# Graph-network stack on one core: the second hop's weights folded into the first's, its node features made by VectorE transposes

## The chip, the cores and the metric

One NeuronCore of one Trainium2 chip runs the kernel. The metric is device microseconds from start to end of an execution. The kernel before took 709.7 us, the median of three runs from 709.64 to 709.86.

## The reference

The input is 3327 nodes with 64 features and a sparse weighted matrix adj of 3327 x 3327 in float32. Four residual layers follow each other; each takes a layer norm and a relu of x, runs its own graph network on it, and adds the result to x. Together they multiply by a matrix made from adj eight times. These eight sweeps are numbered k = 0 to 7 in the kernel. The change concerns the third layer, sweeps k = 3, 4 and 5:

```python
w = left_weights * A                      # both are adj: the squares of adj
for W, b in ((W0, b0), (W1, b1), (W2, b2)):
    x = w @ x
    x = x @ W.T + b
```

The other sweeps are two gated graph units (k = 0, 1, on adj itself), a ranked-neighbour layer (k = 2, on weights made from a mask of adj) and two dense hops with tanh (k = 6, 7, on adj itself).

## The kernel before

**Tiling.** The nodes are padded to 26 blocks of 128 and split in two halves of 13 blocks, s = 0 and 1, which lie side by side on the partition axis: features of half 0 on partitions 0 to 63, of half 1 on 64 to 127. The 13 block positions are cut into four chunks c = 0 to 3 of 3, 3, 3 and 4 blocks, so 384, 384, 384 and 512 columns. Chunks 0 and 1 are group 0, chunks 2 and 3 are group 1. [...]One tile holds one block of 128 source nodes against one group of target nodes: 768 KB for group 0, 896 KB for group 1. Twenty slots hold such tiles, and SyncE's DMA queue fills them (L369).

**Sweeps.** For one source tile and one target chunk, a "unit", TensorE runs in L571 two products, one for each half. Each is shown by the profile as two matmul instructions, since the data are float32. A unit accumulates into a "sum" bank of PSUM, transposed: features on partitions, target nodes on columns. When the last source has been added, the chunk's task after_k starts. Two sweeps share one reading of a tile (`joint`): the order is k = 3 for group 1 beside k = 2, then k = 3 and 4 for group 0, k = 4 and 5 for group 1, k = 5 and 6 for group 0, k = 6 and 7 for group 1, and k = 7 for group 0.

**Order of the work.** The program is a fixed order for each engine, written by a planner. `run` goes through the units, issues loads ahead, prepares the squares six units ahead, and expands the ranked weights three units ahead. After each unit `spend` hands its estimated duration (0.86 us for 512 columns) to the open tasks; a task is a generator whose `yield` says how long to let pass before its next instructions are put into the queues. Nothing is timed on the chip itself: an instruction runs when those before it on its engine are done and its semaphores are there.

**Squares.** For k = 3 to 5, `square` (L402 to L406) squares a tile in place or into a spare half slot. Two of three go to ScalarE (L404). The third goes to VectorE (L406) only if no chunk has an open task; otherwise ScalarE does it too.

**The ranked sweep.** For k = 2 each unit needs a product of a mask with a triangular matrix (L271, `tri`) into a PSUM bank, which ScalarE (L487) or VectorE (L485) turns into weights `e`, before the three bfloat16 terms of the unit run on TensorE. These products, all tasks' products and the sums share the eight PSUM banks: `take` hands out the bank that was given back longest ago, and `give` returns it.

**After a hop.** In `after_hop(k)`, for k = 3 and 4, the sum is copied from PSUM to SBUF in `evacuate` (VectorE, L719, for chunks 0 and 2; ScalarE, L717, for 1 and 3). `dense_to_nodes` multiplies it by the hop's weights: two products for each block (helper `mm`, L271), with nodes on partitions as a result. VectorE adds the bias on its way back to SBUF (L929) and writes y of sweep k + 1, the operand of the next sweep. `bd` holds the weights of the ranked layer and of the three hops as block-diagonal 128 x 128 matrices, places 0 to 3; `brow` holds the three hops' biases as rows (0 to 2).

**Constants.** The task `more_constants` (L204 to L257) loads and builds weights during the first sweeps. Its last steps are the DMAs of bd (L250), w3 (L252) and brow (L254). `transpose_on_vector` (L760 to L769), which sweeps 6 and 7 use, transposes in 32 by 32 squares on VectorE: sixteen instructions of 32 partitions for a chunk.

Of the kernel before, what the change touches and what calls it, by code (L numbers as in the profile page):

```python
# [9 lines left out]
F32 = mybir.dt.float32  # L10
BF16 = mybir.dt.bfloat16
I16 = mybir.dt.int16
AF = mybir.ActivationFunctionType
ALU = mybir.AluOpType
# [30 lines left out]
N, D = 3327, 64  # L45
P = 128
# [8 lines left out]
CWM = 512  # L55
# [10 lines left out]
WL1, WL2, WL3 = 14, 15, 18  # L66
# [25 lines left out]
def upper(n):  # L92
    return slice(n * D, (n + 1) * D)
# [3 lines left out]
def kernel(  # L97
# [9 lines left out]
    nc = tc.nc  # L107

    const = ctx.enter_context(tc.tile_pool(name="const", bufs=1))
    feat = ctx.enter_context(tc.tile_pool(name="feat", bufs=2))  # L110
    work = ctx.enter_context(tc.tile_pool(name="work", bufs=4))
# [11 lines left out]
    bd = const.tile([P, 4, P], F32, name="bd")  # L123
# [5 lines left out]
    both += [both[1][:, :, (CH[c][0] - CH[1][0]) * P:(CH[c][1] - CH[1][0]) * P] for c in PARTS]  # L129
    bcol = const.tile([P, NBIAS], F32, name="bcol")  # L130
    brow = const.tile([P, 4, D], F32, name="brow")
    ident = const.tile([P, P], F32, name="ident")
    make_identity(nc, ident)
    tri = const.tile([P, P], BF16, name="tri")
# [15 lines left out]
    def load_cell(cell):  # L150
        nc.sync.dma_start(out=stage[upper(0), :7 * D].rearrange("p (w f) -> p w f", f=D),
                          in_=weights[:, (W1, W2)[cell]:(W1, W2)[cell] + 7])
        if cell == 0:
            nc.sync.dma_start(out=stage[upper(0), 7 * D:], in_=bias_cols)

    def unfold_cell(cell):

        n = 3 * D + (NBIAS if cell == 0 else 0)
        i, ps = take()
        for h in range(2):  # L160
            nc.tensor.matmul(ps[upper(h), :n], ident[:, :D], stage[:, 4 * D:4 * D + n], start=True, stop=True)
        v = ps[:, :3 * D].rearrange("p (g f) -> p g f", f=D)
        for h in range(2):
            nc.vector.tensor_copy(cells[upper(1 - h), cell, h, 0:3], v[upper(1 - h)])
        if cell == 0:
            nc.vector.tensor_copy(bcol, ps[:, 3 * D:n])
        give(i)

    def fold_cell(cell):

        i, ps = take()
        for n in range(2):
            for h in range(2):
                nc.tensor.matmul(ps[upper(h), upper(n)], stage[:, :D], ident[:, :D], start=True, stop=True)
        tr = work.tile([P, P], F32, name="t2")
        nc.scalar.copy(tr, ps[:, :P])
        give(i)
        yield 1.0
        i, ps = take()
        mm(ps[:, :3 * D], tr, stage[:, D:4 * D])  # L180
        v = ps[:, :3 * D].rearrange("p (g f) -> p g f", f=D)
        for h in range(2):
            nc.vector.tensor_copy(cells[upper(h), cell, h, 0:2], v[upper(h), 0:2])
            nc.vector.tensor_copy(cells[upper(h), cell, h, 3], v[upper(h), 2])
        give(i)
# [4 lines left out]
    def ahead_of_cell(c):  # L190
# [10 lines left out]
        nc.scalar.copy(ahead[c], ps[:, :width(c)])  # L201
        give(i)

    def more_constants():  # L204
        nc.gpsimd.memset(stage, 0.0)
        nc.gpsimd.memset(cells, 0.0)
        for c in range(NC):
            for h in range(2):
                nc.gpsimd.memset(both[c][upper(h), h], 0.0)
        nc.gpsimd.memset(bd, 0.0)  # L210
        yield 5.0
        load_cell(0)
        yield 20.0
        unfold_cell(0)
        yield 1.0

        full = work.tile([P, P], BF16, name="t2")
        nc.gpsimd.memset(full, -TWO7)
        nc.gpsimd.affine_select(out=tri, in_=full, pattern=[[-1, P]], compare_op=ALU.is_gt, fill=0.0,
                                base=0, channel_multiplier=1)  # L220
        nc.gpsimd.affine_select(out=tri, in_=tri, pattern=[[-1, P]], compare_op=ALU.not_equal, fill=TWO7 * TWO7,
                                base=0, channel_multiplier=1)
        nc.gpsimd.memset(tri[:, P - 1:P], 0.0)
        nc.gpsimd.memset(bitsb, BITS)
        nc.gpsimd.memset(lasty, 0.0)
        wide = work.tile([P, P], F32, name="t2")
        nc.gpsimd.memset(wide, 0.0)

        for i, (bi, bh) in enumerate(((BI1, BH1), (BI2, BH2))):
            nc.vector.tensor_add(bsum[:, i], bcol[:, bi:bi + 2], bcol[:, bh:bh + 2])  # L230

        nc.vector.tensor_scalar(wide[0:D], wide[0:D], bcol[0:D, BL1:BL1 + 1], None, op0=ALU.add)
        yield 3.0
        i, ps = take()
        mm(ps[:, :D], wide, ident[:, :D])
        nc.vector.tensor_copy(brow[:, 3], ps[:, :D])
        give(i)
        yield 1.0
        yield from fold_cell(0)
        for c in range(NC):  # L240
            yield 1.0
            ahead_of_cell(c)
        yield 50.0
        load_cell(1)
        yield 20.0
        unfold_cell(1)
        yield from fold_cell(1)
        yield 30.0
        for h in range(2):
            nc.sync.dma_start(out=bd[upper(h), :, upper(h)], in_=weights[:, WL1:WL3])  # L250
            for i in range(2):
                nc.sync.dma_start(out=w3[upper(h), :, i], in_=weights[:, WL3 + (h + i) % 2:NW:2])  # L252
        yield 5.0
        nc.sync.dma_start(  # L254
            out=brow[:, 0:3],
            in_=bass.AP(tensor=bias_rows.tensor, offset=bias_rows.offset, ap=[[0, P], [D, 3], [1, D]]),
        )  # L257


    def blocks(c):  # L260
        return CH[c][1] - CH[c][0]

    def width(c):
        return blocks(c) * P

    def mm(out, lhsT, rhs, start=True, stop=True):


        for h in range(2):
            hs = slice(h * D, (h + 1) * D)  # L270
            nc.tensor.matmul(out[hs], lhsT[:, hs], rhs, start=start, stop=stop)  # L271
# [8 lines left out]
    def take(sums=False, either=True):  # L280


        either = either and not sums
        pool = idle_sums if sums else idle_temps
        if either and idle_sums and (not pool or released[idle_sums[0]] < released[pool[0]]):
            pool = idle_sums
        for c in list(tasks):
            if not pool and c not in running:
                advance(c)
        i = pool.popleft()  # L290
        return i, banks[i]

    def give(i):
        released[i] = max(released) + 1
        (idle_sums if i < 4 else idle_temps).append(i)

    def nodes(c):

        return feat.tile([P, blocks(c), 2, D], F32, name=f"y{c}")
# [4 lines left out]
    def groups(t):  # L304
        return t.rearrange("p b s d -> p (b s) d")
# [4 lines left out]
    def view(ps, c):  # L310
        return ps[:, :width(c)].rearrange("p (b f) -> p b f", f=P)
# [5 lines left out]
    def advance(c):  # L317
        running.add(c)
        try:
            tasks[c][1] = next(tasks[c][0])  # L320
        except StopIteration:
            del tasks[c]
        running.discard(c)
# [23 lines left out]
    y = [[None] * NC for _ in range(8)]  # L347
    after = [None] * 8
# [365 lines left out]
    def evacuate(acc, c, busy=False):  # L714
        m = work.tile([P, CWM], F32, name="t2")[:, :width(c)]
        if c % 2 or busy:
            nc.scalar.copy(m, acc[0][1][:, :width(c)])  # L717
        else:
            nc.vector.tensor_copy(m, acc[0][1][:, :width(c)])  # L719
        give(acc[0][0])  # L720
        return m

    def dense_to_nodes(ft, w, c):

        i, ps = take()
        v = view(ps, c)
        for b in range(blocks(c)):
            mm(v[:, b, :], ft[:, b * P:(b + 1) * P], bd[:, w - WL1, :])
        return i, v
# [30 lines left out]
    def transpose_on_vector(h, c):  # L760

        for s in range(2):
            to = both[c][:, s].rearrange("p (b q n) -> p b q n", q=4, n=32)
            for q in range(4):
# [3 lines left out]
                if q % 2:  # L768
                    yield 1.5  # L769

    def evacuate_stacked(acc, c):
        nc.scalar.copy(both[c][upper(0), 0], acc[0][1][upper(0), :width(c)])  # L772
        nc.vector.tensor_copy(both[c][upper(1), 1], acc[1][1][upper(1), :width(c)])  # L773
        for i in {acc[0][0], acc[1][0]}:
            give(i)
# [142 lines left out]
        yield 15.0  # L918
        add_row(c, 2)

    def after_hop(k):
        def done(c, acc):
            m = evacuate(acc, c)
            yield 0.8
            v = dense_to_nodes(m, WL2 + k - 3, c)
            yield 0.8
            yk = nodes(c)
            n = 2 * blocks(c)
            nc.vector.tensor_tensor(groups(yk), v[1].rearrange("p b (s d) -> p (b s) d", d=D),  # L929
                                    brow[:, k - 3:k - 2, :].to_broadcast([P, n, D]), ALU.add)  # L930
            give(v[0])
            y[k + 1][c] = yk
        return done

    def after_5(c, acc):
        m = evacuate(acc, c)
# [21 lines left out]
    def after_7(c, acc):  # L958
# [8 lines left out]
        g0, g1 = CH[c]  # L967
        nc.scalar.dma_start(out=out[:, g0:g1], in_=xs[:, g0:g1])

    after[:] = [after_0, after_1, after_2, after_hop(3), after_hop(4), after_5, after_6, after_7]  # L970


    alone(0, 0, sweep=2, lag=5)
# [59 lines left out]
```

## Time and profile before

| what | value |
|---|---|
| median of three runs | 709.7 us |
| the profiled execution, its own time | 709.73 us |
| its span from first to last instruction | 707.8 us |
| TensorE matmuls busy | 682.0 us, 96% of the span |
| VectorE busy | 338.3 us, 48% |
| ScalarE busy | 268.3 us, 38% |
| HBM read | 199.45 MB, 283 GB/s over the span |
| granted TensorE clock | 1.0 |

The page gives for each group of instructions the line, the engine, what is written and read, the number of instructions, the busy time, the mean of one, and the idle time of the engine before them with what ended it. PE is TensorE, DVE is VectorE, ACT is ScalarE, POOL is GpSimd, and SPq is SyncE's queue. Several products share the helper line L271, so the operand names (`bd`, `tri`, `ident`) tell them apart. Two products on the two halves of TensorE's columns run at the same time, so the busy time of a group is less than its number times its mean.

### The profile page before, as it was taken

To read this page: it belongs to the slowest core of one execution; us is meant where nothing else is said; L and a number is where in the kernel's file an instruction comes from. 1 tells how busy PE (TensorE), PEld (TensorE's weight loads), DVE (VectorE), ACT (ScalarE), POOL (GpSimd) and SP (SyncE) were. 2 spreads that over 40 slices of the span, in tenths; PEclk is the share of its full clock that TensorE was granted. 3 is DMA by queue.
4 is the path that set the end of the run, shared out by engine and by line. 5 is a ranking of instruction groups with operands and counts; after the bars stand their busy time and mean duration, and the time that the engine had idled before them with its cause. 6 is when DMAs were issued, how large, how long until landed. Compare 5 with 4: busy or idle time off the path is not lost.

```text
span 707.8 us, 12613 instructions
## 1 busy us (share of the span) xinstructions
PE 682.0 (96%) x5128; PEld 354.7 (50%) x5128; DVE 338.3 (48%) x688; ACT 268.3 (38%) x415; POOL 76.1 (11%) x114
## 2 busy tenths in 40 slices
PE   1999999999999999999999999999999999999997
PEld 1454666643546686546444444334444444334464
DVE  7566735634997889747442104221271565005101
ACT  1014100212137878898997125740166600000101
POOL 4300000002291323011100000000010000000000
PEclk9999999999999999999999999999999999999999
DMA  9999996089688943783899559953998399917991
GB/s 341 401 385 405 406 405 230 1 343 376 209 277 302 329 154 107 249 271 126 275 372 341 208 213 408 405 207 113 384 362 271 110 398 405 406 65 279 402 401 37
DMA packets 68549, 201.31 MB, mean 284 GB/s; under 512 B 7228, under 2 KB 8228, under 8 KB 68492
## 3 DMA queue, kind: packets, MB, share of 16 engines
q1 hardware_dynamic: 65596, 199.46, 76.0%
q8 instruction: 40, 0.66, 0.4%
q10 hardware_dynamic: 720, 0.85, 0.3%
q0 software_dynamic: 2176, 0.20, 0.2%
q14 instruction: 17, 0.14, 0.0%
HBM read 199.45 MB, written 0.85 MB: 283 GB/s over the span
## 4 chain that ended last, share of the span: by engine, by line
PE 56%; DMA 1%; DVE 1%; ACT 0%; issue 0%; POOL 0%; ACTq 0%; DVEq 0%; SPq 0%; POOLq 0%
PE sum L571 52%; PE temp L271 3%; PE temp L738 1%; DMA adj<-in_adjT 1%; DMA out<-xs 1%; DVE both L773 0%; ACT both L772 0%; POOL st L793 0%; DVE xs L966 0%; ACT t L963 0%; DVE e L485 0%; PE sum L271 0%; ACT t L717 0%; DVE y L797 0%; DVE y L789 0%
## 5 line engine op out<-in xcount | busy, mean ns | idle before, releaser
L571 PE MATMUL sum<-adj,y 128*64 128x384 f32 (+3 forms) x3016 | 532.0, 501 | 1.6 <-DMA adj<-in_adjT 0.8
L571 PEld LDWEIGHTS sum<-adj,y 128*64 128x64 f32 x3016 | 229.1, 137 | 248.2 <-issue 222.6
L404 ACT ACTIVATE adj<-adj 128x768 f32<-128x768 f32 (+1 forms) x174 | 142.6, 891 | 49.0 <-PE sum L571 25.0
L430 DVE TENSOR_SCALAR adj<-adj 128x768 bf16<-128x768 f32 (+3 forms) x208 | 114.7, 600 | 39.2 <-PE temp L506 31.2
L772 ACT COPY both<-sum 64x384 f32<-64x384 f32 (+3 forms) x17 | 8.1, 478 | 197.0 <-PE sum L571 191.4
L571 PE MATMUL sum<-e,both 128*64 128x384 bf16 (+1 forms) x624 | 73.6, 339 | 0.5 <-DVE e L485 0.5
L487 ACT ACTIVATE e<-temp,bitsb 128x384 int16<-128x384 f32 (+1 forms) x120 | 67.4, 607 | 14.1 <-PE temp L271 8.3
L773 DVE COPY both<-sum 64x384 f32<-64x384 f32 (+3 forms) x17 | 9.7, 569 | 113.6 <-ACT both L772 112.4
L406 DVE TENSOR_TENSOR adj<-adj 128x768 f32<-128x768 f32 (+1 forms) x34 | 32.6, 1009 | 53.9 <-DMA adj<-in_adjT 31.6
L793 POOL TENSOR_TENSOR st<-st,mhalf 128x6 f32<-128x6 f32 (+1 forms) x16 | 24.0, 1498 | 290.6 <-DVE st L791 290.6
L271 PE MATMUL temp<-adj,tri 128*64 128x384 bf16 (+1 forms) x332 | 51.1, 341 | 1.3 <-DVE e L485 1.2
L571 PEld LDWEIGHTS <-both 128*64 128x64 bf16 x624 | 41.0, 110 | 19.3 <-issue 7.0
L435 POOL DMA_DIRECT2D adj<-totals x52 | 33.1, 638 | 51.5 <-PE temp L271 49.1
L485 DVE TENSOR_SCALAR e<-temp 128x384 int16<-128x384 f32 (+1 forms) x46 | 28.3, 617 | 20.8 <-ACT e L487 10.9
L271 PEld LDWEIGHTS <-tri 128*64 128x64 bf16 x416 | 28.5, 110 | 17.6 <-issue 9.9
L767 DVE STREAM_TRANSPOSE both<-y 32x96 f32<-32x96 f32 (+1 forms) x128 | 35.6, 278 | 2.9
L719 DVE COPY t<-sum 128x384 f32<-128x384 f32 x8 | 4.4, 556 | 60.5 <-PE sum L571 60.5
L506 PE MATMUL temp<-adj,behind 128*64 128x384 bf16 x208 | 30.3, 339 | 0.9 <-DVE adj L430 0.7
L506 PEld LDWEIGHTS <-behind 128*64 128x64 bf16 x208 | 17.0, 110 | 17.6 <-issue 15.9
L717 ACT COPY t<-sum 128x384 f32<-128x384 f32 (+1 forms) x8 | 4.2, 528 | 54.4 <-PE sum L571 54.4
L929 DVE TENSOR_TENSOR y<-temp,brow 128x384 f32<-128x384 f32 (+1 forms) x8 | 4.7, 591 | 29.6 <-PE temp L271 29.6
L824 PE MATMUL temp<-both,cells 128*64 128x384 f32 (+1 forms) x68 | 17.2, 520 | 0.0
(121 smaller groups left out, 316.2 us busy)
## 6 DMA issues: line engine op xcount, KB each, us to landing
adj<-in_adjT SPq DMA_DIRECT2D x130, 768.0 KB, 8.9
adj<-in_adjT SPq DMA_DIRECT2D x104, 896.0 KB, 12.0
xs<-in_x SPq DMA_DIRECT2D x1, 640.0 KB
adj<-totals POOLq DMA_DIRECT2D x26, 3.0 KB, 4.7
adj<-totals POOLq DMA_DIRECT2D x26, 3.5 KB, 4.2
out<-xs ACTq DMA_DIRECT2D x2, 192.0 KB
out<-xs ACTq DMA_DIRECT2D x1, 256.0 KB
stage<-in_weights SPq DMA_DIRECT2D x2, 112.0 KB, 13.0
```

The costliest lines, as they stand in the source:

```text
L271: nc.tensor.matmul(out[hs], lhsT[:, hs], rhs, start=start, stop=stop)
L404: nc.scalar.activation(sq, v, AF.Square)
L406: nc.vector.tensor_tensor(sq, v, v, ALU.mult)
L430: nc.vector.tensor_scalar(t.mask.view[:rows, half], t.view()[:rows, half], 0.0, None, op0=ALU.not_equal)
L435: nc.gpsimd.dma_start(out=t.mask.view[P - 1:P], in_=totals[t.g][t.q:t.q + D + 1:D, :])
L485: nc.vector.tensor_scalar(wide[:, s], ps[:, :w], BITS, 0.0, op0=ALU.add, op1=ALU.max)
L487: nc.scalar.activation(wide[:, s], ps[:, :w], AF.Relu, bias=bitsb)
L506: nc.tensor.matmul(counts[c][1][s * D:(s + 1) * D, :w], behind[:, NQ - 1 - t.q:NQ - 1 - t.q + D], t.mask.view[:, s, t.cols(c)], start=firs ...
L571: nc.tensor.matmul(acc[h][1][h * D:(h + 1) * D, :w], yq[h], rhs[h], start=first and n == 0, stop=last and n == len(terms) - 1)
L767: nc.vector.transpose(to[at:at + 32, :, q], h[q * 32:(q + 1) * 32, :, s, f * 32:(f + 1) * 32])
L793: nc.gpsimd.tensor_tensor(st[:, 3, :n], st[:, 2, :n], mhalf[:, :n], ALU.pow)
L824: nc.tensor.matmul(ps[upper(1 - s), :w], cells[:, cell, s, g, :], both[c][:, s], start=True, stop=True)
```

## The change

Sweep 4 is linear, with no function between the hops: (w(w x W0 + b0) W1 + b1) equals w(w x (W0 W1) + b0 W1) + b1, with the W transposed as in the reference. So the change multiplies the second hop's weights into the first's once, and then the second hop's sums need only its bias and a transpose. Everything else is as before.

- `fold_hops` runs at the end of `more_constants`, 22 us of planner time after brow's DMA is issued. It turns the three bias rows into columns (six products, a ScalarE copy of 128 x 384), multiplies b0 by W1 (two products) and writes the result over row 0 of brow, copies b1 as a column to `hopcol` (VectorE, both), and calls `product`, which transposes W0 (two products, a ScalarE copy), multiplies by W1 (two products), and writes over place 1 of bd (ScalarE).
- `after_3` is the old after_hop for k = 3.
- `after_4` calls `sums_to_nodes`: ScalarE copies the sum to SBUF and adds the bias column, for all four chunks, and VectorE makes the node layout with sixteen transposes of 32 partitions. No product of TensorE and no PSUM bank is used.

```diff
+    hopcol = const.tile([P, 2], F32, name="hopcol")
...
+    def product(i, j):
+
+        n, ps = take()
+        mm(ps[:, :P], bd[:, i, :], ident)
+        tr = work.tile([P, P], F32, name="t2")
+        nc.scalar.copy(tr, ps[:, :P])
+        give(n)
+        yield 1.0
+        n, ps = take()
+        mm(ps[:, :P], tr, bd[:, j, :])
+        nc.scalar.copy(bd[:, i, :], ps[:, :P])
+        give(n)
+        yield 1.0
+
+    def fold_hops():
+
+        i, ps = take()
+        for n in range(3):
+            for h in range(2):
+                nc.tensor.matmul(ps[upper(h), n * P:(n + 1) * P], brow[:, n], ident, start=True, stop=True)
+        cols = work.tile([P, CWM], F32, name="t2")
+        nc.scalar.copy(cols[:, :3 * P], ps[:, :3 * P])
+        give(i)
+        yield 1.0
+
+        i, ps = take()
+        mm(ps[:, :D], cols[:, :P], bd[:, 2, :D])
+        nc.vector.tensor_copy(brow[:, 0], ps[:, :D])
+        nc.vector.tensor_copy(hopcol[:, 0:1], cols[:, P:P + 1])
+        give(i)
+        yield 1.0
+        yield from product(1, 2)
...
+        yield 22.0
+        yield from fold_hops()
...
+    def sums_to_nodes(acc, c, bias):
+
+        m = work.tile([P, CWM], F32, name="t2")[:, :width(c)]
+        nc.scalar.activation(m, acc[0][1][:, :width(c)], AF.Identity, bias=hopcol[:, bias:bias + 1])
+        give(acc[0][0])
+        yield 0.8
+        v = m.rearrange("p (b q n) -> p b q n", q=4, n=32)
+        yk = nodes(c)
+        for s in range(2):
+            for f in range(2):
+                at = s * D + f * 32
+                for q in range(4):
+                    nc.vector.transpose(yk[q * 32:(q + 1) * 32, :, s, f * 32:(f + 1) * 32], v[at:at + 32, :, q])
+                yield 1.2
+        return yk
...
-    def after_hop(k):
-        def done(c, acc):
-            m = evacuate(acc, c)
-            yield 0.8
-            v = dense_to_nodes(m, WL2 + k - 3, c)
-            yield 0.8
-            yk = nodes(c)
-            n = 2 * blocks(c)
-            nc.vector.tensor_tensor(groups(yk), v[1].rearrange("p b (s d) -> p (b s) d", d=D),
-                                    brow[:, k - 3:k - 2, :].to_broadcast([P, n, D]), ALU.add)
-            give(v[0])
-            y[k + 1][c] = yk
-        return done
+    def after_3(c, acc):
...
+    def after_4(c, acc):
+        y[5][c] = yield from sums_to_nodes(acc, c, 0)
```

More of the change, by code (lines that the diff above doesn't have):

```diff
@@ L919, in after_2 @@
         add_row(c, 2)
-    def after_hop(k):
-        def done(c, acc):
-            m = evacuate(acc, c)
-            yield 0.8
-            v = dense_to_nodes(m, WL2 + k - 3, c)
-            yield 0.8
-            yk = nodes(c)
-            n = 2 * blocks(c)
-            nc.vector.tensor_tensor(groups(yk), v[1].rearrange("p b (s d) -> p (b s) d", d=D),
-                                    brow[:, k - 3:k - 2, :].to_broadcast([P, n, D]), ALU.add)
-            give(v[0])
-            y[k + 1][c] = yk
-        return done
+    def after_3(c, acc):
+        m = evacuate(acc, c)
+        yield 0.8
+        v = dense_to_nodes(m, WL2, c)
+        yield 0.8
+        yk = nodes(c)
+        n = 2 * blocks(c)
+        nc.vector.tensor_tensor(groups(yk), v[1].rearrange("p b (s d) -> p (b s) d", d=D),
+                                brow[:, 0:1, :].to_broadcast([P, n, D]), ALU.add)
+        give(v[0])
+        y[4][c] = yk
+    def after_4(c, acc):
+        y[5][c] = yield from sums_to_nodes(acc, c, 0)
     def after_5(c, acc):
@@ L968, in after_7 @@
         nc.scalar.dma_start(out=out[:, g0:g1], in_=xs[:, g0:g1])
-    after[:] = [after_0, after_1, after_2, after_hop(3), after_hop(4), after_5, after_6, after_7]
+    after[:] = [after_0, after_1, after_2, after_3, after_4, after_5, after_6, after_7]
     alone(0, 0, sweep=2, lag=5)
```

## The prediction

> **What bounds the kernel now.** I read the page first, then the idle time of TensorE by stretch and by waiting, then the form of each instruction concerned, then the timeline of the places that the change touches.
>
> ```profile
> PE 682.0 (96%) x5128; PEld 354.7 (50%) x5128; DVE 338.3 (48%) x688; ACT 268.3 (38%) x415; POOL 76.1 (11%) x114
> ...
> PE   1999999999999999999999999999999999999997
> ...
> PEclk9999999999999999999999999999999999999999
> ```
>
> TensorE is busy from the second slice to the last, at an even clock. So a product removed is time gained wherever nothing else is nearly late, and a product added is time lost unless TensorE waits there anyway. Stretches of 5 to 12 us show where it waits (columns: busy us of PE, PEld, DVE, ACT, POOL; clock, DMA share, GB/s):
>
> ```profile
> 220.00:225.00 5.00, 5.00 (x41) 2.66 (x38) 3.92 (x8) 3.43 (x8) 0.00 (x0) 1.00 1.01 338
> 225.00:230.00 5.00, 4.78 (x73) 3.62 (x73) 4.87 (x10) 4.18 (x9) 0.00 (x0) 1.00 0.89 319
> 230.00:235.00 5.00, 3.80 (x62) 2.88 (x59) 4.83 (x11) 3.29 (x6) 0.45 (x1) 1.00 1.00 396
> 235.00:240.00 5.00, 4.85 (x54) 3.67 (x55) 4.79 (x12) 3.50 (x8) 2.23 (x2) 1.00 1.02 377
> ...
> 440.00:450.00 10.00, 10.00 (x58) 3.79 (x56) 5.10 (x6) 10.00 (x13) 0.00 (x0) 1.00 1.03 406
> 478.00:490.00 12.00, 12.00 (x82) 5.18 (x80) 1.81 (x3) 0.59 (x1) 0.00 (x0) 1.00 0.09 19
> ```
>
> At the second hop's ends (428 to 435 and 478 to 488) TensorE never rests. From 225 to 240, where the ranked sweep of group 0 starts, it is idle 0.22 + 1.20 + 0.15 = 1.57 us and VectorE is the full engine. Who TensorE waited for from 220 to 240 (total, times, longest):
>
> ```profile
> PE temp L271 <- DVE e L485: 0.9, 1, 0.9
> PE sum L271 <- DVE e L485: 0.3, 1, 0.3
> PE sum L271 <- DVE adj L836: 0.2, 1, 0.2
> ```
>
> L271 with `tri` reads nothing that L485 writes; it waits for the PSUM bank that L485 reads.
>
> **What the Trainium skill says.** "ScalarE: Activation LUTs", section "Table sets: the hidden batching unit": identity and copy are in every set. The trace agrees as far as it goes: copies, relus, squares, sigmoids and tanhs mix here with two table loads (1283 ns each) in all; Identity itself is not shown. "VectorE: DVE Perf Modes", section "The three transpose paths": VectorE transposes in 32 by 32 blocks alone; here L767 needs sixteen instructions for a chunk. "Perfetto Trace Analysis", section "Optimizing Scalar/DVE Operations": every instruction there has a fixed overhead, so many small ones are dear; 270 ns for 32x96 against 557 ns for a whole 128x384 agrees. The same page, section "Matmuls", wants products to rotate through PSUM banks so that evacuation overlaps; the waits above are where this rotation runs out.
>
> **The change part by part.**
>
> *Removed from TensorE.* The timeline around the first two ends:
>
> ```profile
> 427.71 2.43 PE L571 MATMUL sum<-adj,y 128*64 128x384 f32 x14
> 429.97 0.83 PE L271 MATMUL temp<-bd,t 128*64 128x128 f32 x12
> 430.62 4.25 PE L571 MATMUL sum<-adj,y 128*64 128x384 f32 x24
> ```
>
> From the start of the dense products to the next unit is 0.65 us, which agrees with the chain's 0.66. By the distance of the units' starts, less a plain unit (0.645 us for 384 columns, 0.86 for 512), the four pieces cost 0.66, 0.65, 0.68 and 0.87 us: 2.86 us off a TensorE that had no rest there.
>
> *Added to TensorE, the fold.* Twelve such instructions of 128 columns take 0.66 us. Six products for the bias columns are twelve instructions, 0.66. The two products of 64 columns for b0 W1 are four; 24 of that size take 0.70 us (L738), so 0.12. `product` has four products of 128 columns, eight instructions, 0.44. Sum 1.22 us.
>
> *Where the fold lies.* brow's DMA is issued at 193.5 us and lands 6.8 us later (200.3), so its data are no wait. The 22 us are planner time. Counting units of 0.645 us, and ranked ones of about 0.8, from the units next to that DMA, they end just behind the first ranked unit after sweep 1's last sum (that ends at 219.6). So the four steps stand at about 223 to 228, amid chunk 0's and 1's gated units.
>
> *The fold's waits.* The product by W1 waits for ScalarE's copy of 128x384 (0.48 us), the last product for one of 128x128 (0.27); each follows about 1.1 us of other TensorE work, and ScalarE has one to three L487 of 0.58 us ahead of it. A copy lands 1.1 to 2.2 us after its product. So each waits 0 to 1.1 us; I take 0.3 each, 0.6 in all, bounds 0 and 2.2. All of TensorE's queue stands behind such a wait, and behind TensorE the e of ScalarE and VectorE. A third ScalarE copy (0.27) has no early reader. VectorE gets 0.23 (128x64, L236) and 0.15 us (128x1, like L166 of 128x13).
>
> *What absorbs it.* TensorE idles 1.57 us from 226 to 235.5 anyway. But VectorE, busy without a gap from 224.9 on, shifts by its 0.38 us, and some of its L485 wait for L271 products that now come later: that of 231.65 had a lead of only 0.3 us. So between 0 and 1.57 us comes back; I take 0.6, near a third. Fold in all: 1.22 + 0.6 - 0.6 = 1.2 us, bounds -0.4 and +3.4.
>
> *ScalarE and VectorE at the hop's ends.* L719 of chunks 0 and 2 (0.56 each) leaves VectorE. ScalarE takes all four with a bias pointer: by L829, 0.58 for 384 and 0.69 for 512 columns against 0.48 and 0.58 of L717. L929 goes (3 x 0.56 + 0.69 = 2.37 us), and sixteen transposes come: 4.3 us a chunk at 0.270, 4.8 for chunk 3 at 0.303, so 17.8 us, counted as nothing because VectorE is half idle and the result is not due. Chunk 0's y is first read at 441.4, now about 440.1, and can be done by 428.9 + 0.6 + 4.3, some 434, as it stands ahead of the L406 squares in VectorE's queue. Chunk 1's, from 433, is read at 459; chunk 2's, from 478, at 492.5; chunk 3's, from 486, at 501.6. The least cover is 6 us; without it each microsecond late is one lost.
>
> *Squares.* The longer tasks also push squares to ScalarE. At 433.8 its queue goes on with fifteen L404 behind chunk 1's copy; the nearest were done 2.3 us before TensorE's unit. TensorE now arrives 1.3 us earlier, the copy 0.66 earlier and 0.1 longer: 2.3 - 1.3 + 0.56, about 1.6 us left. The planner's third square at 436 (1.2 us, L406) probably moves to ScalarE; the unit that needs it had 6 us, the next 3.9 or more. Price 0; without this cover about 1 us.
>
> *DMA.* No transfer is added or moved. After 430 every tile lands at least 7.7 us before its first unit, except two in the last sweep (3.75 and 7.58 us). TensorE comes at most 2.9 us earlier there, and slots come free earlier too: no wait.
>
> *Sum.* Against the profiled execution: 709.73 - 2.86 + 1.2 = 708.1 us. It lies 0.03 us from the median of the three, so the same holds for that.
>
> **The rivals.**
>
> *The fold is free.* If TensorE's idle 1.57 us swallows all of its 1.22 and the copies come in time, the time is 709.73 - 2.86 = 706.9. For it: the wait follows within 10 us. Against: VectorE's late items themselves depend on products that shift.
>
> *The fold eats the gain.* With both copies at their worst (2.2) and 0.6 absorbed, the fold costs 2.8 and the time is 709.7; with one, 708.6. About 709.1 in the middle. For it: ScalarE is 4.18 us busy of 5 there, and a copy stands behind the expansions. A result hidden behind DMA would also look like this; the landing times speak against it.
>
> *The fold holds up the bank rotation, and the kernel is slower.* From 223 to 243, four more `take` calls shorten the rotation just where L271 already waits for L485's banks. If each costs one wait like the longest (0.9 us), the fold costs 1.22 + 3.6 = 4.8 and the time is 711.7. It decides from waits of 1.64 us in all (2.86 - 1.22), and passes +0.2% at 3.06. Against: the fold's own banks are given back after one short copy.
>
> **How the numbers follow.** 0.2% is 1.4 us, about what a measurement of this kernel can tell from no change; faster means under 708.3. Chances: forecast 0.45 (707.4 to 708.7, four fifths of it under 708.3), free fold 0.22, gain eaten 0.22, rotation 0.11. Faster: 0.36 + 0.22 = 0.58. Same: 0.09 + 0.22 = 0.31. Slower: 0.11. The range takes in the first three cases and the fold's bounds as far as they are likely, from 706.7 to 709.8.
>
> **What would show it.** Right: the dense products of L271 on `bd` fall by 52 instructions, and the units' starts at 430, 435, 479 and 488 close up; L929 is left with four; 64 more transposes of about 270 to 303 ns, none of which TensorE waits for; the fold within 222 to 230 with 1.2 us of products and short waits for ScalarE; the start of sweep 4 about 1.2 us later than now, its successors about 1.7 us earlier. Wrong: waits of TensorE on transposes (y) or on L404 between 437 and 445, a table load beside Identity, a start of sweep 4 later by more than 2 us or not at all.

## The result and the profile after

The changed kernel takes 707.68 us (median of ten runs, 707.23 to 708.49) against 709.74 us for the kernel before (ten runs beside them, 708.95 to 710.53). The ratio is 0.9973, with a 95% interval from 0.9964 to 0.9981: 1.9 us less, 1.3 to 2.6. The profiled execution took 707.41 us with a span of 705.5 us. The forecast was 708.1.

The page of the changed kernel (a part of the shares, of the slices, and of the groups; lines after L204 have moved by 36 to 52, so L571 is now L607, L271 is L307, L404 is L440, L485 is L521, L487 is L523):

```profile
PE 680.6 (96%) x5100; PEld 362.5 (51%) x5100; DVE 351.7 (50%) x747; ACT 271.3 (38%) x421; POOL 75.7 (11%) x114
...
PEclk9999999999999999999999999999999999999999
...
L440 ACT ACTIVATE adj<-adj 128x768 f32<-128x768 f32 (+1 forms) x175 | 143.6, 892 | 47.3 <-PE sum L607 24.6
...
L819 DVE STREAM_TRANSPOSE y<-t 32x96 f32<-32x96 f32 (+1 forms) x64 | 17.8, 278 | 25.2 <-ACT t L810 24.3
```

TensorE has 28 instructions less: 52 dense products gone, 24 of the fold added. The 64 transposes keep VectorE busy for 17.8 us, and TensorE never waits for one of them. One square has moved to ScalarE (175 instead of 174).

The first hop end of sweep 4, on TensorE's timeline (start, duration, instructions):

```profile
426.73 10.70 PE L607 MATMUL sum<-adj,y 128*64 128x384 f32 x62
```

Before, twelve products on `bd` stood between 429.97 and 430.62, and again at 434.7. Now 62 instructions of the sweep follow each other without a break. The stretches shown before, with the same columns:

```profile
225.00:230.00 5.00, 4.74 (x79) 3.99 (x77) 4.24 (x10) 3.81 (x9) 0.00 (x0) 1.00 0.93 320
230.00:235.00 5.00, 4.88 (x74) 3.72 (x71) 4.83 (x10) 3.18 (x7) 0.00 (x0) 1.00 0.93 310
235.00:240.00 5.00, 3.94 (x44) 2.84 (x42) 4.79 (x13) 4.25 (x9) 1.71 (x2) 1.00 1.03 392
...
478.00:490.00 12.00, 12.00 (x64) 4.29 (x61) 8.86 (x32) 3.75 (x5) 0.00 (x0) 1.00 0.21 66
```

From 225 to 240 TensorE still rests for 0.26 + 0.12 + 1.06 = 1.44 us (1.57 before): the idle time has hardly shrunk, most of it only lies later. Between 478 and 490 VectorE works 8.86 us instead of 1.81 us beside a TensorE that is as full as before. TensorE's waits from 220 to 240:

```profile
PE sum L307 <- DVE e L521: 0.9, 1, 0.9
PE sum L307 <- DVE adj L888: 0.3, 1, 0.3
```

None of them is for a copy of the fold. The fold itself, on TensorE's timeline:

```profile
223.51 0.87 PE L224 MATMUL sum<-ident,brow 128*64 128x128 f32 x10
...
225.47 0.28 PE L307 MATMUL temp<-bd,t 128*64 128x64 f32 x2
...
227.31 0.41 PE L307 MATMUL temp<-ident,bd 128*64 128x128 f32 x4
...
229.52 0.41 PE L307 MATMUL temp<-bd,t 128*64 128x128 f32 x4
```

and the two ScalarE copies that these wait for:

```profile
224.72 0.48 ACT L226 COPY t<-sum 128x384 f32<-128x384 f32 x1
...
228.11 0.26 ACT L210 COPY t<-temp 128x128 f32<-128x128 f32 x1
```

The first copy ends at 225.20 and is read at 225.47; the second ends at 228.37 and is read at 229.52. Other work of TensorE's queue stands between, so neither is a wait.

**Where the time went.** The start of a unit in the changed kernel, less the start of the same unit before, is the clearest account. Up to 217 us it varies from one execution to the next by up to 1.5 us, with the same code. Nearly all of this arises at 18 to 21 us. Units of 384 columns start 1.28 us apart at first, and 0.645 us apart from the moment at which the trace's record of TensorE's clock begins, at full speed: at 17.97 us in the changed kernel, at 18.16 before, at 21.06 in e5 below. In all fourteen traces of this document, counted from the kernel's first unit, what follows is late by half the difference between these moments, within 0.02 us: for e5 this gives 1.49, and its units at 100 us are 1.48 late. From 18 to 21 us the same sweep reads so in the changed kernel and in e5 (the clock's column says 1.00 also where its record has not begun):

```profile
18.00:21.00 3.00, 3.00 (x20) 1.26 (x18) 2.47 (x4) 0.00 (x0) 2.82 (x5) 1.00 1.04 403
```

```profile
18.00:21.00 3.00, 3.00 (x12) 1.17 (x10) 2.44 (x4) 0.00 (x0) 2.82 (x5) 1.00 1.04 403
```

The rest arises at one tile's landing at 212 us. From 217 us on the differences repeat within some hundredths, so I read everything from there:

```
unit at (us, before)        217    232.6   285    341    430.6   435.4   479.6   488, end
after less before (us)    -0.12   +1.06  +0.51  +0.63   -0.02   -0.68   -1.36   -2.23
```

The fold costs 1.18 us where it stands. 0.53 us comes back in one step at 285 us, far behind it, and 0.10 of that is lost again by 300 us; so the fold nets 0.63 + 0.12 = 0.75 us. The four hop ends bring 0.65, 0.66, 0.68 and 0.87: 2.86 us. Together 2.1 us.

### The profile page after: what moved, and what is told of

The parts are those of the page before. It is cut to its first block, busy times and chain, and to the rows that moved or that the text cites. A ratio compares the mean times of both kernels' runs of the same rounds, so it can differ in the third digit from the quotient of the medians.

```text
span 705.5 us, 12624 instructions
## 1 busy us (share of the span) xinstructions
PE 680.6 (96%) x5100; PEld 362.5 (51%) x5100; DVE 351.7 (50%) x747; ACT 271.3 (38%) x421; POOL 75.7 (11%) x114
## 4 chain that ended last, share of the span: by engine, by line
PE 84%; DVE 9%; ACT 4%; issue 1%; DMA 1%; SPq 0%; ACTq 0%; DVEq 0%
PE sum L607 70%; PE temp L307 5%; ACT adj L440 4%; DVE adj L466 3%; PE temp L542 2%; PE temp L876 2%; PE sum L307 1%; PE temp L774 1%; PE sum L876 1%; DVE e L521 1%; DMA bd<-in_weights 1%; DVE both L825 1%; DVE adj L901 1%; DVE st L842 0%; DVE t L836 0%
## 5 line engine op out<-in xcount | busy, mean ns | idle before, releaser
L607 PE MATMUL sum<-adj,y 128*64 128x384 f32 (+3 forms) x3016 | 533.6, 501 | 0.8 <-DVE y L849 0.6
L607 PEld LDWEIGHTS sum<-adj,y 128*64 128x64 f32 x3016 | 233.7, 137 | 246.3 <-issue 220.9
L440 ACT ACTIVATE adj<-adj 128x768 f32<-128x768 f32 (+1 forms) x175 | 143.6, 892 | 47.3 <-PE sum L607 24.6
L607 PE MATMUL sum<-e,both 128*64 128x384 bf16 (+1 forms) x624 | 78.4, 339 | 0.5 <-DVE e L521 0.4
L523 ACT ACTIVATE e<-temp,bitsb 128x384 int16<-128x384 f32 (+1 forms) x117 | 66.1, 606 | 15.0 <-PE temp L307 9.9
L307 PE MATMUL temp<-adj,tri 128*64 128x384 bf16 (+1 forms) x332 | 56.8, 341 | 0.5 <-DVE e L521 0.2
L607 PEld LDWEIGHTS <-both 128*64 128x64 bf16 x624 | 46.5, 110 | 15.5 <-issue 2.2
L307 PEld LDWEIGHTS <-tri 128*64 128x64 bf16 x416 | 33.4, 110 | 15.3 <-issue 7.4
L521 DVE TENSOR_SCALAR e<-temp 128x384 int16<-128x384 f32 (+1 forms) x49 | 30.1, 617 | 21.1 <-ACT e L523 10.5
L819 DVE STREAM_TRANSPOSE y<-t 32x96 f32<-32x96 f32 (+1 forms) x64 | 17.8, 278 | 25.2 <-ACT t L810 24.3
L523 ACT ACTIVATE e<-sum,bitsb 128x384 int16<-128x384 f32 (+1 forms) x28 | 16.6, 599 | 2.5 <-PE sum L307 2.0
```

What stands on the lines that cost most here:

```text
L440: nc.scalar.activation(sq, v, AF.Square)
L521: nc.vector.tensor_scalar(wide[:, s], ps[:, :w], BITS, 0.0, op0=ALU.add, op1=ALU.max)
L523: nc.scalar.activation(wide[:, s], ps[:, :w], AF.Relu, bias=bitsb)
L607: nc.tensor.matmul(acc[h][1][h * D:(h + 1) * D, :w], yq[h], rhs[h], start=first and n == 0, stop=last and n == len(terms) - 1)
```

## The experiments

Kernels of one batch ran on one chip, whose kernel before had a median of 710.33 us (first four experiments), 710.17 (e5 to e8), 709.65 (e9 to e11) and 710.57 (e12). A quotient of the medians differs from the ratio given by up to 0.0007. The units' starts are always compared with the one trace of the kernel before.

### The fold alone

The kernel before, with the fold put in at the same place and its results written where nobody reads them:

```diff
+        mm(ps[:, :P], tr, bd[:, j, :])
+        nc.scalar.copy(tr, ps[:, :P])
...
+        mm(ps[:, :D], cols[:, :P], bd[:, 2, :D])
+        nc.vector.tensor_copy(cols[:, 3 * P:3 * P + D], ps[:, :D])
...
+        yield 22.0
+        yield from fold_hops()
```

> The fold alone in the kernel before; its results go to spare places and are not used, so the output is the reference's. Theory (the fold costs its products, 1.2 us, where it stands, and some 0.5 us comes back at 285 us, where another PSUM bank falls to the sum): +0.7 us. Forecast's own figure: +1.2 us. Rival (TensorE's idle time from 226 to 235 swallows the fold): 0. Rival (the fold holds up the bank rotation): over +1.6 us.

711.19 us, ratio 1.0013 (1.0005 to 1.0021): 0.9 us (0.4 to 1.5). The units are 1.19 us later at 232.6 than at 217, and 0.77 us later at 341. The fold alone shows the same two steps, with the same sizes, as the fold in the changed kernel: the return at 285 belongs to it and not to the hop ends.

### The changed kernel without the fold

The product of the weights and the bias columns are left out, so sweep 4 uses the first hop's weights alone and a bias of zero at the second hop.

```diff
+        nc.gpsimd.memset(hopcol, 0.0)
...
-        yield 22.0
-        yield from fold_hops()
```

> The changed kernel without the fold: the product of the weights and both bias columns are left out, so its features after the third layer are wrong and its time is that of the hop's ends alone. Theory: the dense products' 2.86 us in full, so 2.9 us under the kernel before. If the hop's ends bring less than they free (waits for transposes or squares): 1.5 to 2.5 us under it. If the gain came from VectorE and ScalarE: not bound to 2.86.

707.32 us, ratio 0.9960 (0.9948 to 0.9972): 2.8 us less. The starts are within 0.07 us of those before from 217 to 428, and then come 2.86 us earlier in four steps. So the two parts of the change add up: -2.86 here, +0.75 for the fold.

### Only the banks' rotation

The kernel before, with four banks taken and given back at the place of the fold, and not one instruction more:

```diff
+        yield 22.0
+        for n in range(4):
+            i, ps = take()
+            give(i)
+            yield 1.0
```

> The kernel before with four takes of a PSUM bank, each given back at once, at the fold's place: no instruction is added, only the order of the banks moves on by four. Theory (rotation brings 0.5 us back at 285 us): 0.5 us under the kernel before, and the first unit of sweep 3 on chunk 3 starts 0.65 us behind that on chunk 2, not 1.18. Rival (the 0.5 us comes from the later arrival of TensorE alone): no change.

710.13 us, ratio 0.9998 (0.9990 to 1.0006). The total was no different, but the trace was: from 217 to 232 the units fall back by 0.6 to 0.8 us though nothing was added, and part of it is a new wait of 0.3 us for a bank that VectorE's L807 reads. TensorE's idle time between the same units (219 to 240 us) grows from 1.57 to 1.77 us. At 285, 0.54 us comes back in one step, and 0.21 us of the loss are left at 341. I had expected 0.5 us under the kernel before and got half of the mechanism: the return at 285 comes with the rotation alone, without any product, but the rotation also costs about as much at its own place.

The line where the return arises, kernel before and kernel after:

```profile
283.81 0.99 PE L571 MATMUL sum<-adj,y 128*64 128x384 f32 x4
284.99 1.08 PE L571 MATMUL sum<-adj,y 128*64 128x512 f32 x4 [0.19 <-DVE e L485]
```

```profile
284.85 1.85 PE L607 MATMUL sum<-adj,y 128*64 128x384 f32 x8
```

These are the first units of sweep 3 for chunks 2 and 3. Before, chunk 3's sum starts 1.18 us after chunk 2's, and it starts when VectorE has read an expansion's product out of the bank that the sum takes. On VectorE's timeline of the kernel before, that is:

```profile
284.39 0.55 DVE L485 TENSOR_SCALAR e<-sum 128x384 int16<-128x384 f32 x1
```

It ends at 284.94, 0.05 us before the unit. After, the two units stand 0.65 us apart. In the program's order of banks, the one that this sum takes was last read by VectorE (L485) in the kernel before, in the one without the fold and in those whose fold stands elsewhere (e5 and e6, below), and none of these has the return; it was last read by ScalarE, which had finished earlier, in every kernel with a fold or a rotation at 223 us, and all of these have it. That TensorE merely comes later is not the reason: e5, e6, e7 and e9 come to this place 1.4 to 6.6 us late, without a return.

### The dense products kept

The changed kernel, with the old products put back at the hop ends; their result is not read.

```diff
         v = m.rearrange("p (b q n) -> p b q n", q=4, n=32)
+        i, _ = dense_to_nodes(m, WL2 + 1, c)
+        give(i)
```

> The changed kernel with the second hop's dense products put back on TensorE; nobody reads them. Theory (the gain is TensorE's products and nothing else): 2.9 us over the changed kernel, so 0.7 us over the kernel before. Rival (the gain is the relief of VectorE's bias add and copies, or of the wait for them): near the changed kernel's time, 2 us under the kernel before.

710.77 us, ratio 1.0009 (1.0002 to 1.0016). The units are 0.77 us later than before at 217, 1.53 at 341, and 1.53 to 1.56 until the end: all four steps of the gain are gone, and the 0.76 us of the fold stay. The gain is TensorE's products alone; L929's leaving VectorE brings nothing, and the transposes cost nothing.

### The fold later

```diff
-        yield 22.0
+        yield 99.0
         yield from fold_hops()
```

> The changed kernel with the fold 99 us of planner time after brow's DMA instead of 22, so at about 300 us, amid the ranked sweep of group 1, where TensorE hardly waits. Theory (at 223 us half of the fold comes back, because the banks' order moves on by four there): the units behind it start 1.2 us or more later than before the fold, not 0.6. Rival (the fold costs 0.6 us wherever it stands): 0.6 us. Read from the trace, by the units' starts against the kernel before.

One run, 709.33 us. The units are 1.40 us late at 217 and at 285, with the wait of 0.19 us as before, and 2.61 at 341: the fold, now between 309 and 317 us, costs 1.21 us. There, without idle time of TensorE and with no return behind it, the sum of products (1.22) is paid to the hundredth. The hop ends again bring 2.87.

### The fold at the very start

bd and brow are loaded on ScalarE's queue at the start, the fold runs before the first unit, and ScalarE makes VectorE's two copies:

```diff
+    for h in range(2):
+        nc.scalar.dma_start(out=bd[upper(h), :, upper(h)], in_=weights[:, WL1:WL3])
...
+    for _ in fold_hops():
+        pass
     for c in (0, 0, 1, 0, 1, 2, 1, 2, 3, 2, 3, 3):
```

> The changed kernel with bd and brow loaded from ScalarE's queue at the start and the fold run there, with ScalarE's copies in place of VectorE's two, while TensorE waits 15 us for its first operand. Theory: the fold then costs nothing on TensorE, so 0.6 us under the changed kernel and 2.6 us under the kernel before. Rival (224 KB more at the head of a saturated DMA start delay the first tiles): 0 to 1 us over the changed kernel.

712.08 us, ratio 1.0033 (1.0020 to 1.0046): slower by 2.3 us. I had taken TensorE's first 15 us for free. Its timeline:

```profile
11.76 1.55 PE L231 MATMUL temp<-ident,brow 128*64 128x128 f32 x12 [11.76 <-DMA brow<-in_bias_rows]
...
20.47 1.54 PE L789 MATMUL sum<-ident,y 128*64 128x128 f32 x12 [4.60 <-DVE y L847]
21.80 2.77 PE L605 MATMUL sum<-adj,y 128*64 128x384 f32 x8
```

brow, issued at 2.8 us behind bd, landed at 11.8. The first layer norm had to wait for that too: the fold's tiles come from the same four buffers as its own, and VectorE waits 5.2 us for ScalarE to have read the last of them. The first unit starts at 21.80 us instead of 16.34. Later the fold's cost at 223 us is gone, as expected, but 5.4 us had been paid for it.

### Three hops folded, at the start

If the second hop's products are worth 2.86 us, the third's might be had too: fold W2 into W0 W1 as well, and only transpose at the third hop's ends (for chunk 0 by a product with the identity).

```diff
+        yield from product(2, 3)
...
+        mm(ps[:, P:2 * P], bd[:, 3, :], cols[:, P:2 * P])
...
-        v = dense_to_nodes(m, WL2 + 2, c)
-        yield 0.8
-        residual(v, c)
+        if c == 0:
...
+        else:
+            t = work.tile([P, 4, 2, D], F32, name="t2")[:, :blocks(c)]
+            yield from squares_to_nodes(m, c, t, 0.8)
+            nc.vector.tensor_tensor(flat(xchunk(c)), flat(xchunk(c)), flat(t), ALU.add)
```

> As the one with the fold at the start, and the third hop's weights are folded too: the third hop's sums get VectorE's transposes for chunks 1 to 3, and for chunk 0 the same products with the identity, because its y is due within about 1 us. Theory (TensorE's products are what counts, while VectorE has room): 0.66 + 0.68 + 0.87 = 2.2 us under the fold at the start, 4.8 under the kernel before. Rival (the layer norm behind the transposes comes late, and TensorE waits for y of sweep 6): 0 to 2 us under the fold at the start.

711.74 us, ratio 1.0021 (1.0014 to 1.0028). The start loses 5.3 us in the same way. Behind it the third hop brings 0.68 + 0.87 - 0.28 + 0.65 - 0.60 = 1.3 us, by the steps between the units: the last 0.6 goes at 586 us, where TensorE waits for a VectorE copy (`both`) that stands behind transposes.

The same with brow ahead of bd, with room of its own for the fold, and in one go:

```diff
-        tr = work.tile([P, P], F32, name="t2")
+        tr = both[3][:, 1, :P]
...
-        cols = work.tile([P, CWM], F32, name="t2")
+        cols = both[3][:, 0]
```

> As the three hops folded at the start, but brow is loaded ahead of bd, the copies take the room of a chunk's stacked features, which is idle then, instead of the layer norm's four buffers, and the fold runs in one go. Theory (the 5.4 us lost at the start were waits for those buffers and for brow's late landing, not the fold): sweep 0 starts at 16.3 to 17 us again, and the time is 1.5 to 2.1 us under the changed kernel, some 4 under the kernel before. Rival (the loads at the head are themselves the delay): over the changed kernel by 2 us or more.

709.13 us, ratio 0.9993 (0.9985 to 1.0000). The buffers are no longer in the way and the first unit starts at 19.39 us, still 3.05 us late. The load of x's first chunk, time from issue to landing, in the changed kernel and in this one:

```profile
xs<-in_x SPq DMA_DIRECT2D x1, 192.0 KB, 2.5
```

```profile
xs<-in_x SPq DMA_DIRECT2D x1, 192.0 KB, 5.5
```

brow's load is issued at 0.81 us, in the same moment as x's; with bd's the queue moves 0.23 MB in 688 small packets. In e6, where bd was issued at 1.40 (here at 1.36) and brow at 2.81 us, x's load still landed after 2.5 us. What differs beside x's load is brow's, so I put the 3.0 us down to it; the whole kernel waits for x's load. In none of the three ways tried was the start a free place for the fold.

### Each transposition twice

To find the cover of the transposes, the changed kernel makes each of them twice:

```diff
-                for q in range(4):
+                for q in (0, 1, 2, 3, 0, 1, 2, 3):
```

> The changed kernel with each of the 64 transposes made twice, 17.8 us more of VectorE. Theory (6 us or more of cover for each chunk): no unit of sweep 5 or 6 starts later than in the changed kernel. Rival (VectorE's time is on the path): up to 4 us later behind 440 us. Read from the units' starts.

One run, 715.8 us; I had expected no unit to start later. VectorE's timeline, and TensorE's:

```profile
431.22 18.86 DVE L819 STREAM_TRANSPOSE y<-t 32x96 f32<-32x96 f32 x64 [15.54 <-ACT t L810]
450.12 8.98 DVE L442 TENSOR_TENSOR adj<-adj 128x1024 f32<-128x1024 f32 x9
```

```profile
451.40 10.97 PE L607 MATMUL sum<-adj,y 128*64 128x512 f32 x42 [4.29 <-DVE adj L442]
```

TensorE comes to wait not for y but for VectorE's squares, which are queued behind the transposes: against the kernel before, the units are 0.40 us late at 435.4, 4.87 at 446.5 and 7.73 at 449.5. Only the first step, 4.47 us, is the wait. The second, 2.86 us, comes while TensorE is busy, at half its clock:

```profile
451.00:457.00 6.00, 5.60 (x16) 1.93 (x18) 6.00 (x7) 4.90 (x6) 0.00 (x0) 0.50 1.03 407
```

The record has 0.5 from 450.3 to 457.1 us. Of the fourteen traces only this one and e11's (below) have a rest of TensorE of more than 0.92 us behind 26 us (4.30 and 2.72), and only these two have such a stretch before the end of TensorE's work. That the rest brings it is what this suggests; no run varies it alone.

In the changed kernel the same place reads, with the first square by itself:

```profile
430.14 9.08 DVE L819 STREAM_TRANSPOSE y<-t 32x96 f32<-32x96 f32 x32 [15.54 <-ACT t L810]
439.25 1.23 DVE L442 TENSOR_TENSOR adj<-adj 128x1024 f32<-128x1024 f32 x1
```

The first square ends at 440.48, and the unit that needs it, by the program's order, starts at 445.85. So the cover of VectorE's work is 5.4 us; doubling adds 18.86 - 9.08 = 9.78 us, and 9.78 - 5.4 = 4.4 agrees with the wait. ScalarE's squares have less; the nearest in the changed kernel between 436 and 460 us is this:

```profile
437.92 1.05 ACT L440 ACTIVATE adj<-adj 128x1024 f32<-128x1024 f32 x1
```

It ends at 438.97, 0.87 us before its unit at 439.84.

### The rotation turned back

If the return at 285 us came from the count of banks taken, six takes (four of the fold and two bare ones) should restore the old order:

```diff
         yield from fold_hops()
+        for n in range(2):
+            i, ps = take()
+            give(i)
+            yield 1.0
```

> The changed kernel with two more takes of a PSUM bank, given back at once, behind the fold's four: six banks rotate there, so every bank is again where it stood in the kernel before. Theory (the 0.6 us that came back at 285 us is the order of the banks): the first units of sweep 3 stay 1.2 us behind those without the fold, none of it comes back. Rival (it is TensorE's later arrival): 0.6 us comes back as in the changed kernel. Read from the units' starts.

One run, 709.01 us. The step at 285 is there all the same (2.53 to 2.00 us late), and behind it this kernel runs 1.45 to 1.5 us behind the changed one throughout, as it already did at 217. The count was the wrong idea: `give` orders the banks too, and with six takes ScalarE is again the last reader of the bank in question.

### Three hops folded at the fold's own place

As in the version at the start, but fold_hops stays 22 us of planner time behind brow's load, and VectorE makes the copies:

```diff
+        yield from product(2, 3)
...
         mm(ps[:, :D], cols[:, :P], bd[:, 2, :D])
         nc.vector.tensor_copy(brow[:, 0], ps[:, :D])
-        nc.vector.tensor_copy(hopcol[:, 0:1], cols[:, P:P + 1])
+        mm(ps[:, P:2 * P], bd[:, 3, :], cols[:, P:2 * P])
+        nc.vector.tensor_copy(hopcol[:, 0:1], ps[:, P:P + 1])
```

> The changed kernel with the third hop's weights folded in too, at the fold's own place (six more products, 0.66 us), and VectorE's transposes at the third hop's ends for chunks 1 to 3. Theory (TensorE's products are what counts): 2.2 us of dense products less 0.66 of fold and 0.6 to 0.9 of late features, as the version at the start showed, so 0.6 to 0.9 us under the changed kernel. Rival (late features take all of it): the changed kernel's time or above.

708.22 us, ratio 0.9973 (0.9961 to 0.9984), no better than the change itself. TensorE's and VectorE's timelines show why:

```profile
233.34 0.44 PE L309 MATMUL temp<-t,bd 128*64 128x128 f32 x4 [2.73 <-DVE brow L233]
```

```profile
231.80 0.55 DVE L839 TENSOR_REDUCE st<-xs 128x6 f32<-128x384 f32 x1
...
233.07 0.22 DVE L233 COPY brow<-temp 128x64 f32<-128x64 f32 x1
```

I had put the second bias product behind VectorE's copy out of the same bank. That copy lasts 0.22 us, but it stood behind the expansions and a layer norm in VectorE's queue, and all of TensorE's queue stood behind the product: 2.73 us. Here too TensorE then runs at half its clock, by the record from 234.6 to 238.0 us:

```profile
234.70:238.00 3.30, 3.30 (x42) 2.70 (x40) 2.26 (x5) 1.21 (x3) 0.88 (x1) 0.50 0.72 226
```

From 217 to 341 us this fold nets 2.88 us. How that divides between the wait and the clock, no run separates.

With both products ahead of the copies, the copies on ScalarE, and two bias rows turned instead of three:

```diff
         mm(ps[:, :D], cols[:, :P], bd[:, 2, :D])
-        nc.vector.tensor_copy(brow[:, 0], ps[:, :D])
         mm(ps[:, P:2 * P], bd[:, 3, :], cols[:, P:2 * P])
-        nc.vector.tensor_copy(hopcol[:, 0:1], ps[:, P:P + 1])
+        nc.scalar.copy(brow[:, 0], ps[:, :D])
+        nc.scalar.copy(hopcol[:, 0:1], ps[:, P:P + 1])
```

> As the three hops folded at the fold's own place, with both products of the biases ahead of the copies that read their bank, those copies on ScalarE, and two bias rows turned instead of three (0.22 us less). Theory (the 2.7 us wait there was for VectorE's copy, which stood behind a layer norm, and not for TensorE's work): the fold costs 0.4 us of products more than the changed kernel's, the third hop's ends bring 1.3, so some 0.9 us under the changed kernel and 2.9 under the kernel before. Rival (any larger fold is lost in this stretch): the changed kernel's time or above.

705.90 us (705.19 to 706.85), ratio 0.9936 (0.9922 to 0.9949): 4.5 us less than before (3.6 to 5.5). TensorE's waits from 220 to 240 us:

```profile
PE temp L309 <- DVE e L523: 0.7, 1, 0.7
PE sum L309 <- DVE adj L893: 0.2, 1, 0.2
```

The wait of 2.7 us is gone, and the clock stays full. By the starts of the units, this larger fold nets 0.33 us from 217 to 341, the second hop brings 2.86 and the third 1.32 (1.48 us early at 488, 2.80 at 586 and to the end): 3.85 us in all against 2.11 for the change. I had expected this fold to cost 0.4 us more than the smaller one, and it nets 0.42 less. TensorE rests less beside it, 0.97 us between the units of 219 and 240 against 1.44; why, no run shows.

## Why the prediction was right, and where its sum was off

**Right, within a hundredth: the removal.** The forecast had 0.66, 0.65, 0.68 and 0.87 us for the four ends; measured are 0.65, 0.66, 0.68 and 0.87. e4 shows that these are TensorE's products and nothing else.

**Right: place and products of the fold.** It lies at 223.4 to 230.1 us (forecast 223 to 228), and its products cost 1.21 us where nothing covers them (e5; forecast 1.22). e1 and e2 show that the two parts add.

**Mis-sized: the fold's waits.** The forecast had 0.6 us of waits for ScalarE's copies; there were none. It took a copy to land 1.1 to 2.2 us after its product. The first landed about 0.7 us after (225.20, with the bias products' end near 224.5), because only the rest of one expansion stood ahead of it.

**Mis-sized, and the true cause missed: what comes back.** The forecast let TensorE's idle time from 226 to 235.5 us absorb 0.6 us. That idle time shrank by 0.13 us only (1.57 to 1.44). Instead 0.53 us came back at 285 us (0.43 with the drift behind it) through another order of the banks, of which the forecast has no word. So 1.22 + 0.6 - 0.6 = 1.2 was right for the time up to 283 us by luck, with two wrong terms that cancel, and 0.45 too much for the whole: 0.75 us by the traces of the changed kernel, e1 and e4. With this term the sum is 709.73 - 2.86 + 0.75 = 707.6 us, against 707.68 measured. How far the rotation's own price and the idle time share in the 1.18 us stays open: the rotation alone costs 0.6 to 0.8 us there (e3), the fold with its rotation 1.18, so the products added only some 0.5 to it. Against e3 the fold does fill 0.33 us of idle time (1.77 to 1.44); the rest no run separates.

**The rivals.** The free fold falls: it costs 1.2 us on the spot. That the result lies between its 706.9 and the forecast is due to the return at 285, not to idle time. The eaten gain falls with the waits for copies. The rotation does hold TensorE up, as the third rival said, but by 0.6 to 0.8 us in all and not 3.6, and it gives 0.54 back; the point from which it would have decided (1.64 us) was not reached. e11 shows that the danger was real in another form: one copy at the wrong place of VectorE's queue holds TensorE up for 2.7 us, and 3.4 us at half clock follow.

**Right: VectorE and ScalarE at the ends.** Transposes of 270 and 303 ns, 17.8 us in all, and Identity of 565 to 582 ns for 384 and 687 ns for 512 columns are as forecast. ScalarE has two table loads of 1283 ns as before, so what "ScalarE: Activation LUTs", section "Table sets: the hidden batching unit", says of identity now holds in this trace too. The third square did move to ScalarE, and nothing waited for it.

**Mis-sized: the cover of ScalarE's squares.** The forecast left 1.6 us; 0.87 is left. It moved the squares behind chunk 1's copy forward by 0.56 us, and they come 0.76 us later (434.56 instead of 433.80), since five squares now stand behind chunk 0's copy and ahead of chunk 1's. It cost nothing, but of these covers it is the narrowest.

**Wrong in its reason: the cover.** The forecast named y of chunk 0 as what is late next when the transposes take longer, with 6 us or more. Its cover is 6.0 us (last transpose to 434.67, first read at 440.70), but the squares that VectorE has queued behind the transposes come first, with 5.4 us (e8). It cost nothing here, but the sentence would have misled whoever made the transposes longer.

**Shown as forecast, but for its size: sweep 4.** It started 0.75 us later by the shift since 217 instead of 1.2, and the end came 2.1 us earlier instead of 1.7.

## What to carry to other kernels

Where one engine is full from end to end, price an edit by the distance of its repeating units' starts in the stretch concerned: the removal came out to the hundredth in this way. An added piece of work is worth looking at beyond its own place: it reorders whatever is handed out in rotation, and it puts its short copies behind whatever stands in an engine's queue, so products that depend on such a copy should be issued as late, and the copy on as empty an engine, as can be. "Before the kernel starts" is not free when everything waits for the first load.

## What the runs showed that I had not expected

- Taking and giving back four PSUM banks, with no instruction added, shifts TensorE's units by 0.6 to 0.8 us at that place and by -0.5 us 55 us later (e3). What counts is which engine last read the bank that a sum takes, and when it was done.
- brow's 96 KB, issued on another queue in the same moment, go with a first load of 192 KB that lands after 5.5 instead of 2.5 us (e9).
- An execution's first 217 us vary by up to 1.5 us with the same code, nearly all of it by when TensorE comes to full speed (17.97 to 21.06 us in the eleven traces whose first unit starts at 16.2 to 16.4), and what follows by some hundredths. A difference of one or two microseconds is read better from one trace, stretch by stretch, than from a few times.
- The two long rests of TensorE were followed by half clock: 4.30 us by 6.8 us of it (e8), 2.72 us by 3.4 us (e11). In e8 this added 2.86 us to a wait of 4.47. Rests of up to 0.92 us, in all traces, were not.
